# A four-layer graph network in fp32: layer 2's weight product by a seven-product scheme over two graphs, softmax weights turned in place, and smaller buffers

## The chip, the cores and the metric

The kernel runs on one core of one Trainium2 chip. The time is that of one execution on the device, in microseconds (us). The kernel before ran three times: median 2760.49 us, from 2757.43 to 2760.59. Engines are named as the profile names them: PE (matrix engine, with PEld for its weight loads), DVE (vector), ACT (scalar), POOL (GpSimd), SP (the queue that issues most DMAs). All data are fp32.

## The reference

There are 128 graphs of 128 nodes with 512 channels, one 128 x 128 weighted adjacency `adj`, and four layers. Each layer adds its result to its input and then normalises the row (`ln`: mean 0, variance 1, over the 512 channels).

```python
# x: (128 graphs, 128 nodes, 512 channels); adj: (128, 128)
# layer 0: A = adj @ x; the whole of it reduces to relu(max over channels of A + b) per node
x = ln(x + relu(max(adj @ x, axis=-1) + b)[..., None])
# layer 1: graph attention
h = x @ W; s1 = h @ a1; s2 = h @ a2
att = softmax(leaky_relu(s1[:, None] + s2[None, :]) * adj)
x = ln(x + elu(att @ h + beta * h))
# layer 2: graph convolution
y = adj @ x
x = ln(x + y @ weight + bias)
# layer 3: attention with 8 heads of 64, masked where adj == 0
q, k, v = x @ Wq + bq, x @ Wk + bk, x @ Wv + bv
x = ln(x + concat_heads(softmax(q @ k.T / 8 + mask) @ v))
```

## The kernel before

**Order of the work.** The kernel is written out as one instruction stream by a planner in Python (`Plan`, L23 to L133). Each stage of the work is a generator that announces what it will use: `dve(us)`, `act(us)`, `pool(us)`, `sp(us, landing)`, a buffer tag, or a mark of another stage. The planner keeps a clock for PE and one for each other engine with the costs that the code gives, and at each moment picks the PE stage with the smallest due place whose marks and buffers are there (L97 to L133). So each engine has one fixed order, and at run time every engine takes its instructions strictly in that order, waiting on semaphores. A stage's due place is `(graph + turns) * 7 + position in the row` (L955 to L960): in one round each graph-stage is done once, for graphs that lie up to some 15 apart.

**PE stages of one graph.** `l0` (L399) is adj x input, one product of 512 columns. `zT` (L503) is four products of 128 columns, `z` (L517 in `product`, called from `l1_out`) four of 512 columns accumulated in one PSUM bank, with the layer-1 weight as the moving operand and the turned data as the stationary one. `yT` (L560) and `y` (L517 again, called from `l2_out`) are the same pair for layer 2: `yT` holds (adj x2) turned, and `y` multiplies it by `w2_sb`. `xT`, or a turn by DMA and DVE, makes layer 3's input stationary.

**q, k, v by seven products.** For layer 3 the weight products of four graphs at a time (a group, GB = 4) are already made from seven products of half-size blocks (`seven`, L682 to L757; the tables `SEVEN` and `WAITS` at L668). The 512 x 512 weight is cut into four blocks, and so are the 512 nodes' data; sums and differences of blocks are made once for the weights (`weight_sums`, L327) and per group for the data (`token_sums`, L590, on POOL). A step is four matmuls of 256 columns. Steps 0, 2, 4, 5 accumulate in one bank (`chain`), step 1 in `first`, steps 3 and 6 in `pair`; between the steps ACT or DVE copy partial sums out, so that step 2 waits for the copy of step 0, step 4 for that of step 2, step 5 for that of step 4, and step 6 for a finished block.

**After `y`.** DVE adds `ps_y` and `x2b` (L605), where POOL has made `x2b = x2 + bias` before (L546). `layernorm` (L351 to L365) is bn_stats and bn_aggr on DVE (L354, L356), three small POOL instructions (L359, L361, L363) and one ACT pass (L365).

**Turns.** `turn` (L367 to L388) transposes a tile without PE: SP writes it to HBM, reads it back with rows regrouped, and DVE transposes 32 x 32 blocks (L386). The destination there is addressed with neighbouring elements four apart, which is 16 bytes. Layer 1's attention (n = 1), layer 3's input (n = 4), the softmax weights `pr` (n = 8, into a tile `turn8` and from there to `pT`) and the head outputs `oT` (n = 4) go this way.

**Softmax and `av`.** `l3_scores` (L794) makes 8 score products, DVE adds the mask (L816) and takes the maximum (L822), ACT makes 8 exponentials (L826); after the turn, `l3_avT` makes 16 half-height products (L880) whose moving operand is `pT[:, e * 4 + f, :]`, 128 elements side by side, and ACT copies them to `oT` (L892).

**PSUM.** Six banks (`mm`) serve all stages but the scores, which have two banks of their own as one tile.

Of the kernel before, what the change touches and what calls it, by code (L numbers as in the profile page):

```python
# [14 lines left out]
P = 128  # L15
# [121 lines left out]
def kernel(  # L137
# [30 lines left out]
        "x0": 2, "x1": 4, "x2": 2, "x2b": 2, "x3": 2, "x3r": 1, "xp": 4, "junk": 1,  # L168
        "s2_bc": 2, "s2_row": 2, "e": 2, "pe": 2, "att": 1, "attT": 2, "zT": 1, "yT": 1, "elu_r": 1,
        "xTh": 3, "T": 1, "st": 4, "qTh": 3, "kTh": 3, "pr": 1, "pT": 2, "oT": 1,  # L170
        "turn1": 2, "turn4": 2, "turn8": 1,
    }
    ps_bufs = {"mm": 6, "sc": 1}
    hbm_bufs = {"s2_hbm": 3, "turn_hbm1": 3, "turn_hbm4": 3, "turn_hbm8": 3, "x3_hbm": 16}
    NV = 2
# [96 lines left out]
    for i in range(NV):  # L272
        t = const.tile([P, GB, H, HD + 1], F32, tag=f"va{i}", name=f"va{i}")
        nc.vector.memset(t, 1.0)
        va_bufs.append(t)
# [13 lines left out]
    def w1_a():  # L289

        yield sp(0.0, 6.5)
        for i in (1, 0):
            junk = yield from get("junk", [P, C], f"wa_junk{i}")
            dg = yield from get("oT", [P, NCC, P], f"wa_diag{i}")
            yield dve(3.9)
            cols = small.tile([P, NCC], F32, tag="cols", name=f"wa_cols{i}")
            for c in range(NCC):
                nc.vector.scalar_tensor_tensor(
                    junk, w1_sb[:, c, :], 1.0, a_bc[i], ALU.mult, ALU.mult, accum_out=cols[:, c : c + 1]
                )  # L300
            nc.vector.tensor_tensor(
                dg,
                ident.unsqueeze(1).to_broadcast([P, NCC, P]),
                cols.unsqueeze(2).to_broadcast([P, NCC, P]),
                ALU.mult,
            )
            plan.give("junk")
            plan.give("xp")
            yield "mm"
            ps = ps_tile("mm", f"ps_wa{i}")  # L310
            yield ("PE", 1.0, 0.0)
            nc.tensor.matmul(ps, ones, dg.rearrange("p c n -> p (c n)"), start=True, stop=True)
            plan.give("oT")
            yield dve(0.7)
            nc.vector.tensor_copy(wa_bc[i], ps)
            plan.give("mm")
            plan.mark(("wa", i))
        yield dve(0.5)
        nc.vector.tensor_scalar(bq_s, bq_col, QS, None, ALU.mult)
        nc.vector.tensor_scalar(beta_id, ident, beta_col, None, ALU.mult)  # L320
        plan.mark("beta_id")
# [5 lines left out]
    def weight_sums(n, w):  # L327

        t = const.tile([P, 3, 2, HALF], F32, tag=f"sums_{n}", name=f"sums_{n}")
        a11, a12, a21, a22 = (w[:, 2 * c : 2 * c + 2, r * HALF : (r + 1) * HALF] for r in range(2) for c in range(2))  # L330
        sums[n] = (a11, a12, a21, a22, t[:, 0], t[:, 1], t[:, 2])
        yield sp(0.0, {"q": 44.0, "k": 52.0, "v": 60.0}[n])
        if n == "q":
            for c in range(NCC):
                yield act(0.6)
                nc.scalar.mul(w[:, c, :], w[:, c, :], QS)
        for dst, x_, y_, op in (
            (t[:, 0], a21, a22, ALU.add),
            (t[:, 1], t[:, 0], a11, ALU.subtract),
            (a21, a11, a21, ALU.subtract),  # L340
            (t[:, 2], a12, t[:, 1], ALU.subtract),
        ):
            yield pool(1.3)
            nc.gpsimd.tensor_tensor(dst, x_, y_, op)
            yield sp(0.0, 0.7)
        plan.mark(("sums", n))
# [20 lines left out]
    def turn(src, tag, place, n, name, kept="turn_hbm{}"):  # L367

        kept = kept.format(n)
        d = yield from get_hbm(kept, [NQ, P, n * Q], f"turn_hbm_{name}")
        yield sp(0.35, {1: 4.0, 4: 5.5, 8: 5.5}[n])
        nc.sync.dma_start(out=d.rearrange("b p x -> p b x"), in_=src.rearrange("p b n r -> p b (n r)"))
        plan.give(tag)
        t = yield from get(f"turn{n}", [P, NQ, n, Q], f"turn_{name}")
        yield sp(0.35, {1: 4.0, 4: 4.0, 8: 5.0}[n])
        nc.sync.dma_start(
            out=t.rearrange("p a n r -> p (a n r)"), in_=d.rearrange("b (c a) x -> (b c) (a x)", a=NQ)  # L380
        )
        if kept.startswith("turn"):
            plan.give(kept)
        dst = yield from place()
        yield dve({1: 0.3, 4: 0.7, 8: 1.25}[n])
        nc.vector.transpose(dst.rearrange("p n (c a) -> p a n c", a=NQ), t)  # L386
        plan.give(f"turn{n}")
        return d  # L388
# [5 lines left out]
    def l0(b):  # L394
# [11 lines left out]
        xp = yield from get("xp", [P, C], f"xp0_{b}")  # L406
        yield act(0.72)
        nc.scalar.activation(xp, xin_b, AF.Identity, bias=rl)
        plan.give("x0")
        if b + sb_bufs["x0"] < B:  # L410
            plan.at(plan.end, load_x(b + sb_bufs["x0"]))
        yield from layernorm(xp, x1, f"0_{b}")
        plan.give("xp")
        s["x1"] = x1
        cols = []
        for i in (1, 0):
            yield ("mark", ("wa", i))
            junk = yield from get("junk", [P, C], f"junk{i}_{b}")
# [3 lines left out]
                junk, x1, 1.0, wa_bc[i], ALU.mult, ALU.mult, accum_out=col  # L422
            )
            plan.give("junk")
# [95 lines left out]
    def l1_out(b):  # L520
# [23 lines left out]
        xb = yield from get("x2b", [P, C], f"x2b_{b}")  # L544
        yield pool(1.28)
        nc.gpsimd.tensor_tensor(xb, x2, bias2_bc, ALU.add)  # L546
        s["x2b"] = xb
        done_x2(b)

    def done_x2(b):  # L550
        st[b]["x2_uses"] = st[b].get("x2_uses", 0) + 1
        if st[b]["x2_uses"] == 2:
            plan.give("x2")

    def l2_yT(b):
        s = st[b]
        x2 = s.pop("x2")
# [5 lines left out]
        done_x2(b)  # L563
        yT = yield from get("yT", [P, C], f"yT_{b}")
        yield act(0.6)
        nc.scalar.copy(yT, ps)
        plan.give("mm")
        s["yT"] = yT
        plan.mark(("yT", b))

    xTh, xsum, heads = {}, {}, {}
    uses = {}
# [22 lines left out]
    def l2_out(b):  # L595
        s = st[b]
        yT = s.pop("yT")
        ps = product(f"y_{b}", lambda c: yT[:, c * P : (c + 1) * P], lambda c: w2_sb[:, c, :])
        plan.give("yT")
        if b == B - 1:  # L600
            plan.give("w")
            plan.give("w")
        xp = yield from get("xp", [P, C], f"xp2_{b}")
        yield dve(0.7)
        nc.vector.tensor_tensor(xp, ps, s.pop("x2b"), ALU.add)  # L605
        plan.give("mm")
        plan.give("x2b")
        x3 = yield from get("x3", [P, C], f"x3_{b}")
        early = b < EARLY
        x3_v = x3 if early else x3.rearrange("p (b n c) -> p b n c", b=NQ, c=Q)  # L610
        yield from layernorm(by_block(b, xp), x3_v, f"2_{b}")
        plan.give("xp")
        g, j = divmod(b, GB)
        half = j // 2
        if j % 2 == 0:
            xTh[g, half] = yield from get("xTh", [P, NCC, 2, P], f"xTh_{g}_{half}")
        if j == 0:
            plan.at(plan.end, token_sums(g))
        if early:
# [8 lines left out]
        place = lambda: made(xTh[g, half][:, :, j % 2, :])  # L628
        s["x3_hbm"] = yield from turn(x3_v, "x3", place, NCC, f"x3_{b}", "x3_hbm")
        plan.mark(("xT", b))  # L630

    def done_x3(b):
        st[b]["x3_uses"] += 1
        if st[b]["x3_uses"] == 2:
            plan.give("x3")
# [18 lines left out]
    def l3_xT(b):  # L654
# [6 lines left out]
        done_x3(b)  # L661
        yield act(0.6)
# [3 lines left out]


    SEVEN = ((0, 0), (1, 1), (5, 5), (2, 3), (4, 4), (6, 2), (3, 6))  # L668
    WAITS = (None, None, 1, 2, 0, None, 3)

    def seven(n):
        bias = {"q": bq_s, "k": bk_col}.get(n)

        def step(t):
# [3 lines left out]
            bank = ("chain", "first", "chain", "pair", "chain", "chain", "pair")[i]  # L678
# [19 lines left out]
            def out(r, c):  # L698

                if n == "v":  # L700
                    return va_bufs[g % NV][:, 2 * c : 2 * c + 2, 4 * r : 4 * r + 4, 0:HD]
# [30 lines left out]
            def half_tile(c):  # L732
                if n != "v":
# [43 lines left out]
    def seven_bufs(n):  # L777
        return lambda t: {"mm": 1 if t % 7 in (0, 1, 3) else 0, **({"va": 1} if n == "v" and t % 7 == 0 else {})}

    def seven_place(n):  # L780
        def at(t):
            g, i = divmod(t, 7)
            order = 14 + i if n == "v" else 2 * i + (n == "k")
            return (GB * g + 7.5 + order * GB / 21) * R
# [3 lines left out]
    def l3_scores(b):  # L788
# [53 lines left out]
        def place():  # L842
            s["pT"] = yield from get("pT", [P, H, P], f"pT_{b}")
            return s["pT"]

        yield from turn(pr_q, "pr", place, H, f"pr_{b}")
        plan.mark(("pT", b))

    def l3_pT(i):
# [11 lines left out]
        s["pT"] = sb_tile("pT", [P, H, P], f"pT_{b}")  # L861
# [10 lines left out]
    def l3_avT(b):  # L872
# [3 lines left out]
        va = va_bufs[b // GB % NV][:, b % GB]  # L876
        ps = ps_tile("mm", f"ps_av_{b}")
        for f in range(NCC):
            for e in range(2):
# [3 lines left out]
                    pT[:, e * 4 + f, :],  # L883
# [3 lines left out]
        if b % GB == GB - 1:  # L887
# [3 lines left out]
        yield act(0.62)  # L891
        nc.scalar.copy(oT.rearrange("p b n c -> p n b c"), ps.rearrange("p (n b c) -> p n b c", n=NCC, b=NQ))  # L892
# [23 lines left out]
    def l3_av(i):  # L916
# [4 lines left out]
        va = va_bufs[b // GB % NV][:, b % GB]  # L921
# [9 lines left out]
        else:  # L931
            if b % GB == GB - 1:
# [23 lines left out]
    turns = {"av": 14.5, "sc": 11.5, "yT": 3, "y": 3, "l0": 0, "zT": 2, "z": 2}  # L956
# [8 lines left out]
    def av_waits(b):  # L965
# [11 lines left out]
        "y": (place("y"), 3.45, lambda b: [("yT", b)], need("mm"), l2_out),  # L977
# [16 lines left out]
    total.update(s2=EARLY, attT=EARLY, xT=EARLY, pT=LATE, avT=B - LATE, av=2 * LATE, **{n: 7 * (B // GB) for n in "qkv"})  # L994
# [4 lines left out]
    for n, w in (("q", wq_sb), ("k", wk_sb), ("v", wv_sb)):  # L999
# [33 lines left out]
```

## Time and profile before

| | |
|---|---|
| median of 3 runs | 2760.49 us |
| the profiled execution: its time, its span | 2759.28 us, 2757.5 us |
| PE busy | 2707.9 us |
| DVE busy | 2248.3 us |
| ACT busy | 1578.1 us |
| POOL busy | 1391.1 us |
| DMA moved | 392.26 MB, mean 142 GB/s |
| `y` products (L517, 1024 records) | 466.7 us |
| q, k, v steps (L690): one group of 256 records, as `ps_q_first` | 60.5 us |

A record is one pass of a matmul: an fp32 matmul leaves two. A line of the profile names the source line, the engine, the operation, destination<-sources, the shapes, the number of records, and then the total busy time, the mean of one in ns, and the idle time of the engine just before. The ends of PE records are modelled and overlap the start of the next, so for PE the distance from start to start is the better duration. In the timeline, the columns are start, duration, engine, line.

### The profile page before, as it was taken

The numbers are of one execution on the slowest core, as the hardware profiler recorded it, in microseconds if no ns is written. First come the engines' busy times: TensorE is split into PE (matmuls) and PEld (weight loads), VectorE is DVE, ScalarE is ACT, GpSimd is POOL, SyncE is SP. The second block draws the span as 40 slices with busy tenths as digits, with TensorE's granted clock in tenths as the row PEclk, the third lists the DMA queues.
The fourth block names the chain that finished last, engine by engine and source line by source line (L and its number), as shares of the span: only waits on it lengthen the run. The fifth ranks groups of instructions, "written<-read, shape, count | busy, mean of one in ns | idle before, by whom it ended". The sixth has DMA issues, their size and how long they took to land.

```text
span 2757.5 us, 43085 instructions
## 1 busy us (share of the span) xinstructions
PE 2707.9 (98%) x13905; PEld 1936.6 (70%) x13905; DVE 2248.3 (82%) x4288; ACT 1578.1 (57%) x4189; POOL 1391.1 (50%) x2192
## 2 busy tenths in 40 slices
PE   6999999999999999999999999999999999999997
PEld 3677767777777777777777777777777777777776
DVE  7668888888888888888888888888888888888866
ACT  3445655655556555556555656555565655555555
POOL 3535445555455555455554555554545544555545
PEclk8999999999999999999999999999999999999998
DMA  3224444544544454445445444445545544454443
GB/s 124 60 72 149 149 144 147 152 150 142 150 146 141 158 147 145 155 142 153 149 138 159 147 148 147 148 147 152 152 137 153 153 142 148 146 156 145 141 148 111
DMA packets 459794, 392.26 MB, mean 142 GB/s; under 512 B 88752, under 2 KB 376624, under 8 KB 459568
## 3 DMA queue, kind: packets, MB, share of 16 engines
q1 hardware_dynamic: 456464, 383.74, 45.6%
q10 hardware_dynamic: 2976, 5.77, 0.6%
q8 instruction: 109, 1.79, 0.3%
q14 instruction: 117, 0.96, 0.1%
q0 software_dynamic: 128, 0.01, 0.0%
HBM read 218.17 MB, written 171.24 MB: 141 GB/s over the span
## 4 chain that ended last, share of the span: by engine, by line
PE 95%; DVE 2%; POOL 1%; DMA 1%; issue 0%; ACT 0%; SPq 0%; POOLq 0%; DVEq 0%
PE ps_y L517 16%; PE ps_z L517 16%; PE ps_v_chain L690 8%; PE ps_k_chain L690 8%; PE ps_q_chain L690 8%; PE ps_sc L794 5%; PE ps_yT L560 5%; PE ps_av L880 4%; PE ps_zT L503 4%; PE ps_q_pair L690 4%; PE ps_v_pair L690 4%; PE psA L399 4%; PE ps_k_pair L690 4%; PE ps_q_first L690 2%; PE ps_v_first L690 2%; PE ps_k_first L690 2%
## 5 line engine op out<-in xcount | busy, mean ns | idle before, releaser
L365 ACT ACTIVATE x<-xp,nmr,rstd 128x512 f32<-128x512 f32 x384 | 311.4, 811 | 348.8 <-POOL nmr L363 347.7
L359 POOL TENSOR_SCALAR ve<-mv 128x1 f32<-128x1 f32 x512 | 124.3, 243 | 732.7 <-DVE mv L356 487.3
L517 PE MATMUL ps_y<-w_sb,yT 128*128 128x512 f32 x1024 | 466.7, 598 | 0.0
L517 PE MATMUL ps_z<-w_sb,zT 128*128 128x512 f32 x1024 | 462.4, 594 | 3.8 <-DVE xp L605 2.6
L826 ACT ACTIVATE pr<-pr,nm 128x128 f32<-128x128 f32 x992 | 384.2, 391 | 120.3 <-DVE nm L822 117.3
L354 DVE BATCH_NORM_STATS2 stats<-xp 128x6 f32<-128x512 f32 x512 | 347.1, 678 | 49.4 <-POOL xp L906 22.2
L517 PEld LDWEIGHTS ps_z<-w_sb,zT 128*128 128x128 f32 x1024 | 194.4, 191 | 211.1 <-issue 202.1
L517 PEld LDWEIGHTS ps_y<-w_sb,yT 128*128 128x128 f32 x1024 | 188.4, 190 | 195.7 <-issue 191.0
L361 POOL TENSOR_TENSOR rstd<-ve,nhalf 128x1 f32<-128x1 f32 x512 | 296.1, 578 | 42.7
L648 POOL TENSOR_TENSOR x3r<-x3r,bv_bc 128x512 f32<-128x512 f32 x128 | 179.1, 1400 | 245.3 <-DMA x3r<-turn_hbm_x 235.2
L386 DVE STREAM_TRANSPOSE pT<-turn_pr 128x1024 f32<-128x1024 f32 x122 | 250.7, 2055 | 0.0
L421 DVE SCALAR_TENSOR_TENSOR junk<-x,wa_bc 128x512 f32<-128x512 f32 x256 | 228.4, 892 | 13.8 <-ACT x L365 12.6
L905 POOL TENSOR_TENSOR xp<-xp,rd 128x512 f32<-128x512 f32 x122 | 127.3, 1043 | 149.0 <-DVE xp L386 93.5
L534 DVE SCALAR_TENSOR_TENSOR xp<-ps_z,x 128x512 f32<-128x512 f32 x128 | 88.4, 691 | 123.0 <-ACT elu_r L530 120.8
L826 ACT ACTIVATION_READ_ACCUMULATOR pr<-pr,nm 128x1 f32 x976 | 184.3, 189 | 0.0
L546 POOL TENSOR_TENSOR x2b<-x,bias_bc 128x512 f32<-128x512 f32 x128 | 164.2, 1283 | 37.4 <-ACT x L365 37.1
L906 POOL TENSOR_TENSOR xp<-xp,x3r 128x512 f32<-128x512 f32 x122 | 169.7, 1391 | 9.6
L816 DVE TENSOR_TENSOR pr<-ps_sc,mask 128x1024 f32<-128x1024 f32 x124 | 151.0, 1218 | 23.7 <-PE ps_sc L794 22.8
L363 POOL TENSOR_SCALAR nmr<-mv,rstd 128x1 f32<-128x1 f32 x512 | 139.6, 273 | 53.0
L530 ACT ACTIVATE elu_r<-ps_z 128x512 f32<-128x512 f32 x128 | 75.3, 589 | 154.7 <-PE ps_z L517 154.5
L794 PEld LDWEIGHTS ps_sc<-kTh,qTh 64*128 64x128 f32 x2048 | 124.2, 187 | 49.2 <-issue 42.6
L503 PEld LDWEIGHTS ps_zT<-attT,x 128*128 128x128 f32 x1024 | 130.6, 193 | 29.7 <-issue 26.6
(148 smaller groups left out, 5816.9 us busy)
## 6 DMA issues: line engine op xcount, KB each, us to landing
turn_hbm_pr<-pr SPq DMA_DIRECT2D x122, 512.0 KB
turn_pr<-turn_hbm_pr SPq DMA_DIRECT2D x122, 512.0 KB
x<-in_x_dram SPq DMA_DIRECT2D x128, 256.0 KB
out_dram<-xp SPq DMA_DIRECT2D x128, 256.0 KB
turn_hbm_x<-x SPq DMA_DIRECT2D x124, 256.0 KB
turn_x<-turn_hbm_x SPq DMA_DIRECT2D x124, 256.0 KB
x3r<-turn_hbm_x SPq DMA_DIRECT2D x124, 256.0 KB
turn_hbm_o<-oT SPq DMA_DIRECT2D x122, 256.0 KB
```

The source lines that it names most:

```text
L354: nc.vector.bn_stats(stats, src)
L361: nc.gpsimd.tensor_tensor(rstd, ve, nhalf, ALU.pow)
L365: nc.scalar.activation(dst, src, AF.Identity, bias=nmr, scale=rstd)
L386: nc.vector.transpose(dst.rearrange("p n (c a) -> p a n c", a=NQ), t)
L421: nc.vector.scalar_tensor_tensor(junk, x1, 1.0, wa_bc[i], ALU.mult, ALU.mult, accum_out=col)
L503: nc.tensor.matmul(ps[:, c * P : (c + 1) * P], s["x1"][:, c * P : (c + 1) * P], attT, start=True, stop=True)
L517: nc.tensor.matmul(ps, lhsT(c), rhs(c), start=(c == 0), stop=(c == NCC - 1))
L648: nc.gpsimd.tensor_tensor(s["x3r"], s["x3r"], by_block(b, bv_bc), ALU.add)
L690: nc.tensor.matmul(ps[:, m, :], lhsT, rhs, start=fresh and m + k == 0, stop=m + k == 2, skip_group_check=not fresh)
L794: nc.tensor.matmul(ps[:, h % 2, f, :], heads["q", g][j // 2][r : r + HD, f, j % 2 * P : (j % 2 + 1) * P], heads["k", g][j // 2][r : r + HD ...
L826: nc.scalar.activation(pr_h[:, i], pr_h[:, i], AF.Exp, bias=nm[:, i : i + 1], accum_out=None if late else den[:, i : i + 1])
L906: nc.gpsimd.tensor_tensor(by_block(b, xp), by_block(b, xp), s.pop("x3r"), ALU.add)
```

## The change

**Layer 2.** `l2_out` goes; `y` becomes `l2_seven`, run once for two graphs in seven steps of two matmuls each (256 columns), with the tables of q, k and v. `yT` holds both graphs of a pair. After the second `yT` copy, `y_sums` makes four differences of 128 x 256 on POOL. `add_bias2` adds the bias to `x2` itself on POOL, after `yT` has been read. Steps 0, 2 and 4 are copied out by ACT and get a half of `x2` added on POOL (`temp`); DVE adds the rest (`finish`, four half adds for each pair). A fourth set of weight sums is made at the start (`y`), and the weight block that the sums replace is overwritten in `w2_sb`.

**Turns.** For the softmax weights, DVE transposes the tile that was loaded in place, all of it side by side. The columns of `pT` then stand in four runs of 32 (`pT[:, :, e * 4 + f, :]`), and the ACT copy to `oT` puts them in order, with neighbours 16 bytes apart.

**Buffers.** `x0` is normalised in place and also takes the unused output of the two row sums of layer 1, so it is held until both are done; before, it was free after the first ACT pass. `x3` lives in an `xp` tile. `v`'s tiles hold two graphs each, three of them instead of two tiles of four. `turn8`, `x2b`, `x3` and `junk` go. q, k, v, the scores and `av` are due one round later.

```diff
-        "x0": 2, "x1": 4, "x2": 2, "x2b": 2, "x3": 2, "x3r": 1, "xp": 4, "junk": 1,
+        "x0": 2, "x1": 4, "x2": 4, "x3r": 1, "xp": 4,
...
-    NV = 2
+    NV = 3
...
-        yield sp(0.0, {"q": 44.0, "k": 52.0, "v": 60.0}[n])
+        yield sp(0.0, {"y": 30.0, "q": 44.0, "k": 52.0, "v": 84.0}[n])
...
-        t = yield from get(f"turn{n}", [P, NQ, n, Q], f"turn_{name}")
+        t = yield from get("pT" if place is None else f"turn{n}", [P, NQ, n, Q], f"turn_{name}")
...
+        if place is None:
+            yield dve(1.25)
+            nc.vector.transpose(t.rearrange("p a n c -> p (a n c)"), t.rearrange("p a n c -> p (a n c)"))
+            return t
...
-        xp = yield from get("xp", [P, C], f"xp0_{b}")
         yield act(0.72)
-        nc.scalar.activation(xp, xin_b, AF.Identity, bias=rl)
-        plan.give("x0")
...
+        nc.scalar.activation(xin_b, xin_b, AF.Identity, bias=rl)
+        yield from layernorm(xin_b, x1, f"0_{b}")
...
-                junk, x1, 1.0, wa_bc[i], ALU.mult, ALU.mult, accum_out=col
+                xin_b, x1, 1.0, wa_bc[i], ALU.mult, ALU.mult, accum_out=col
...
+            if i == 0:
+                plan.give("x0")
...
+    def add_bias2(b):
+
+        x2 = st[b]["x2"]
         yield pool(1.28)
-        nc.gpsimd.tensor_tensor(xb, x2, bias2_bc, ALU.add)
...
+        nc.gpsimd.tensor_tensor(x2, x2, bias2_bc, ALU.add)
+        plan.mark(("x2b", b))
...
+    def y_sums(p):
+
+        t = yield from get("Ty", [P, 3, 2, P], f"Ty_{p}")
+        d = ys[p]
+        b11, b21, b12, b22 = (d["yT"][:, j, 2 * k : 2 * k + 2] for j in range(2) for k in range(2))
+        d["blocks"] = (b11, b21, b22, b12, t[:, 0], t[:, 1], t[:, 2])
+        for i, dst, x_, y_ in ((0, t[:, 0], b12, b11), (1, t[:, 1], b22, t[:, 0]), (2, b12, b22, b12), (3, t[:, 2], b21, t[:, 1])):
+            yield pool(0.72)
+            nc.gpsimd.tensor_tensor(dst, x_, y_, ALU.subtract)
+            plan.mark(("Ty", p, i))
...
+    def l2_seven(t):
+
+        p, i = divmod(t, 7)
+        d = ys[p]
+        w_i, x_i = SEVEN[i]
+        bank = BANKS[i]
+        fresh = i in (0, 1, 3)
+        if fresh:
+            d[bank] = ps_tile("mm", f"ps_y_{p}_{bank}")[:, :HALF]
+        ps = d[bank]
...
+        for k in range(2):
+            nc.tensor.matmul(ps, x_k[:, k], sums["y"][w_i][:, k, :], start=fresh and k == 0, stop=k == 1, skip_group_check=not fresh)
...
+        def temp(j, r):
+            tmp = yield from get("sty", [P, HALF], f"sty_{p}_{i}")
+            yield act(0.36)
+            nc.scalar.copy(tmp, ps)
+            plan.mark(("y", p, i))
+            yield ("mark", ("x2b", 2 * p + j))
+            yield pool(0.72)
+            nc.gpsimd.tensor_tensor(tmp, tmp, half(j, r, "x2"), ALU.add)
...
+        def finish(j, r, key):
+            yield ("mark", ("y", p, key, "b"))
+            yield dve(0.45)
+            bank = d["first" if i == 1 else "pair"]
+            nc.vector.tensor_tensor(xp_half(j, r), as_xp(j, bank), as_xp(j, d.pop(("st", key))), ALU.add)
...
+        if i in (2, 4, 5):
+            keys.append(("y", p, {2: 0, 4: 2, 5: 4}[i]))
+        if i == 6:
+            keys.append(("y", p, "C", 1, 1))
...
-                    pT[:, e * 4 + f, :],
+                    pT[:, :, e * 4 + f, :],
...
-        yield act(0.62)
-        nc.scalar.copy(oT.rearrange("p b n c -> p n b c"), ps.rearrange("p (n b c) -> p n b c", n=NCC, b=NQ))
+        yield act(0.95)
+        nc.scalar.copy(oT.rearrange("p b n (l a) -> p n a b l", a=NQ), ps.rearrange("p (n a b l) -> p n a b l", n=NCC, a=NQ, b=NQ))
...
-    turns = {"av": 14.5, "sc": 11.5, "yT": 3, "y": 3, "l0": 0, "zT": 2, "z": 2}
+    turns = {"av": 15.5, "sc": 12.5, "yT": 3, "y": 3, "l0": 0, "zT": 2, "z": 2}
...
-        "y": (place("y"), 3.45, lambda b: [("yT", b)], need("mm"), l2_out),
+        "y": (
+            lambda t: place("y")(t // 7 * 2 + 1) + t % 7 * 0.3, 0.88, l2_waits,
+            lambda t: {"mm": 1 if t % 7 in (0, 1, 3) else 0}, l2_seven,
+        ),
```

## The prediction

> **What bounds the kernel now.** I read the page first, for busy shares and for the chain that ended last, then the stretches of the span, then PE's timeline in the steady middle.
>
> ```profile
> PE 2707.9 (98%) x13905; PEld 1936.6 (70%) x13905; DVE 2248.3 (82%) x4288; ACT 1578.1 (57%) x4189; POOL 1391.1 (50%) x2192
> ...
> PE 95%; DVE 2%; POOL 1%; DMA 1%; issue 0%; ACT 0%; SPq 0%; POOLq 0%; DVEq 0%
> ```
>
> PE is busy for all but 49.6 us of 2757.5, and 95% of the chain that ended last is PE. The stretches (length, then busy time and records of PE, PEld, DVE, ACT, POOL, then granted clock) say where the 49.6 us lie:
>
> ```profile
> 0.00:60.00 60.00, 35.40 (x92) 17.23 (x93) 41.86 (x111) 21.06 (x40) 17.47 (x34) 0.83 0.41 142
> 60.00:120.00 60.00, 54.30 (x217) 33.44 (x217) 41.09 (x92) 27.51 (x51) 42.31 (x59) 1.00 0.18 47
> 1200.00:1600.00 400.00, 400.00 (x2057) 286.22 (x2056) 339.50 (x636) 234.81 (x632) 200.19 (x320) 1.00 0.48 148
> 2680.00:2760.00 80.00, 60.93 (x446) 52.70 (x444) 50.69 (x83) 39.51 (x109) 44.57 (x58) 0.88 0.36 117
> ```
>
> Some 30 us are at the start, 19 at the end, nothing in between: in the middle PE does not wait, at full clock. So PE work that goes comes off the time one for one, and other engines' work is free until it makes PE wait. The timeline of PE gives prices from start to start:
>
> ```profile
> 1218.81 3.70 PE L517 MATMUL ps_y<-w_sb,yT 128*128 128x512 f32 x8
> 1222.34 1.05 PE L503 MATMUL ps_zT<-attT,x 128*128 128x128 f32 x8
> 1223.23 1.89 PE L690 MATMUL ps_q_pair<-T,wq_sb 128*128 128x256 f32 x8
> 1224.96 3.60 PE L517 MATMUL ps_z<-w_sb,zT 128*128 128x512 f32 x8
> 1228.39 1.89 PE L690 MATMUL ps_k_pair<-T,wk_sb 128*128 128x256 f32 x8
> 1230.12 1.89 PE L690 MATMUL ps_v_chain<-wv_sb,xTh 128*128 128x256 f32 x8
> ```
>
> Here `y` costs 3.53, `z` 3.43 and a step of four 256-column matmuls 1.73. Over 400 to 2600 us the mean of the whole `y` products in the timeline is 3.477, and of steps followed by a step 1.73, so half a step is 0.865. A wide matmul ahead of a 128-column one costs 0.09 more (a step before the scores 1.82, `l0` 0.95 against 0.86).
>
> **The change, part by part.**
>
> *The seven products.* Away go 128 x 3.477 = 445 us. In come 7 x 64 = 448 half steps, 448 x 0.865 = 387.5 us. The order of the changed program has 241 places where a wide product stands before a narrow one, against 208 before; 58 of the 208 were `y`'s and are already in the 3.477, so 241 - 150 = 91 are to be paid at 0.09, 8 us. Sum on PE: 387.5 + 8 - 445 = -49.5 us. All of this is on the path. Weight loads do not take over: the steps of q, k and v load one weight for each 256 columns too, 190 ns (PEld rows of L690) under passes of 0.216.
>
> *What feeds the new steps.* For each pair ACT makes three copies of 256 columns; 128 columns cost it 262 ns (L493), 512 cost 580 (L566), so about 0.37 each, 192 x 0.37 = 71 us. POOL makes four differences and three adds of 256 columns; 512 cost it 1.28 (L546) to 1.40 (L648), so about 0.7 each, 448 x 0.7 = 314 us, and POOL rises from 1391 to 1705 us, 63%. DVE makes four adds of 256 from PSUM; 512 cost 690 ns (L605), 256 cost 424 (L939), so 4 x 0.424 - 2 x 0.690 = +0.32 for each pair, +20 us. None of it is on the path while the steps find their data. Where PE could wait, by the changed order: from the second `yT` to step 2 lie 3.5 to 10.8 us of PE work, median 6.5, for an ACT copy of 0.58, two differences of 0.7 and the hand-overs, about 2.3; from step 4 to step 5 lie 1.73 in 53 pairs of 64 (0.87 in three), for one copy of 0.37; from step 4 to step 6 a median of 4.8, at least 1.9, for copy, POOL add and DVE add, about 1.8 together. Steps 4 and 5 of q stand 1.73 apart as well, with two ACT passes of 0.47 between, and PE does not wait. So bare durations fit; queues in front of ACT, POOL and DVE are what is left. I take 3 us of new waits, from 0 to 30 (0.5 for each pair).
>
> *POOL against DVE.* The timeline shows what more POOL work does to DVE:
>
> ```profile
> 1223.33 1.28 POOL L648 TENSOR_TENSOR x3r<-x3r,bv_bc 128x512 f32<-128x512 f32 x1 [3.42 <-DMA x3r<-turn_hbm_x]
> 1224.09 1.06 DVE L421 SCALAR_TENSOR_TENSOR junk<-x,wa_bc 128x512 f32<-128x512 f32 x1
> 1225.69 0.67 DVE L421 SCALAR_TENSOR_TENSOR junk<-x,wa_bc 128x512 f32<-128x512 f32 x1
> ```
>
> The same row sum takes 1.06 beside a POOL add and 0.67 without. About 800 DVE instructions read two SBUF tensors (L421, L536, L462, L463, L476); 314 us of 2710 are 12% of the time, and a hit waits half of 0.7, which is some 30 us in all. DVE with this and the +20: 2300 us, 85%. Free as long as DVE catches up.
>
> *The turn of the softmax weights in place.* The rows:
>
> ```profile
> L386 DVE STREAM_TRANSPOSE pT<-turn_pr 128x1024 f32<-128x1024 f32 x122 | 250.7, 2055 | 0.0
> L816 DVE TENSOR_TENSOR pr<-ps_sc,mask 128x1024 f32<-128x1024 f32 x124 | 151.0, 1218 | 23.7 <-PE ps_sc L794 22.8
> L438 DVE STREAM_TRANSPOSE s_row<-s 128x32 f32<-128x32 f32 x124 | 23.4, 189 | 0.0
> ```
>
> A turn of 1024 to places 16 bytes apart takes 2055 ns, 1.7 times an add of 1024. The Trainium skill (SBUF — State Buffer, section "Door 1: The DMA port swizzle") says that SBUF works in lines of 16 bytes, and that every access that crosses to a new line pays; by that the in-place turn, side by side, would come down to the 1.2 of the add: 122 x 0.85 = -104 us on DVE. Against it, the one turn that is side by side already, 32 wide, takes 189 ns, which lies on the straight line through the strided ones (373, 1116, 2055 for 128, 512, 1024): by that row the gain is nothing. I take the rule, since 32 elements are too few to tell a slope; DVE is then at 2200 us, 81%, and at 2300 without. The same rule speaks against the copy to `oT`, which now writes 16 bytes apart: at 580 ns now, it could double its slope of 0.83 ns an element, to 1.0 us; +0 to +52 us on ACT, which with the copies comes to 1650 to 1700, 61 to 63%. Neither end is on the path.
>
> *The new form of `pT` for PE.* The moving operand of `av` comes in four runs of 128 bytes. No matmul in the trace reads so. Nearest, the DVE add L816 writes runs of 32 elements at 1218 ns against 1191 for L822, and the ACT copy L892, in runs of 32 too, takes the 580 of L566: no price. Upper bound 25 ns on each of 1952 passes, a fifth of their distance, 49 us; below zero is excluded, as the same columns pass. I take 0.
>
> *Buffers, start and end.* The number of DMAs is the same, and a turn still takes 512 KB out and in. `x0` is held through the normalisation and two row sums, some 10 us in place of 3, with two tiles and a new graph each 21 us: free in the middle. At the start graphs 2 and 3 are loaded only after the row sums of 0 and 1, some 10 us later than now (psA of graph 2 at 17.5 us); PE idles there anyway until 45 us. Against that, the order brings 49 us of PE work before the first q step where it was 42. At the end the last scores stand closer together. I take 0 for both, and 10 us each way. PSUM gets tighter: the chain bank is held for some 20 us of each pair in place of one bank for 3.5, six in all; in the trace PE waits for a bank behind L605 for 2.6 us in total. This is in the 0 to 30.
>
> *Sum.* 2759.3 (profiled execution, 1.8 of it outside the span) - 49.5 + 3 = 2712.8; the median of the runs is 1.2 above the profiled one. Predicted: 2713.
>
> **The rivals.**
>
> *Feeders late, but not by much.* ACT, POOL and DVE stand behind one another between steps 4 and 6, and each has its own queue: eight exponentials hold ACT for 3.1 us. At 0.4 us for each pair, 64 x 0.4 = 26 us: 2736. For it: three engines in a row for a few us of cover. Against: q's steps have the same cover and no wait.
>
> *POOL blocks PE, slower.* POOL takes its instructions in order, and it now makes steps 2, 3, 4 and 6 possible. It stands waiting for `x3r` from DMA for 235.2 us in 77 waits, 3.1 each, up to 5.8; the differences of a pair may stand behind one, and then also behind adds of 1.4. Cover is 6.5 - 2.3 = 4.2 in the median and 1.2 at the least. It decides when PE loses more than 49.5 / 64 = 0.77 us for each pair; at 1.0 it is 2713 - 3 + 64 = 2774. Against: `token_sums` already feeds PE from POOL, with no wait in the middle of the span.
>
> *The gain is eaten, no change.* If the runs of `pT` cost the full 25 ns, 2713 + 49 = 2762, within the bound; or if half steps cost more than half of a step: 0.11 us more on 448 does the same. `l0`, one 512-column matmul in two passes, 0.86 for as many columns as a half step has, speaks against the second.
>
> **How the numbers follow.** PE stays the bound, 2713: 0.74, from 2698 (start and end both better, no waits) to 2727. Feeders late, 2736: 0.13. No change, 2762: 0.06. POOL blocks, 2774: 0.07. A measurement of this kernel can tell about 0.2%, 5.5 us, from no change. Faster: 0.74 + 0.13 = 0.87; same 0.06; slower 0.07. The range of 8 in 10 takes the first case and most of the second: 2698 to 2738.
>
> **What would show it.** PE busy near 2660 and the seven `y` groups summing to about 390 us; PE at full busy time in the middle stretches. In-place turns at 1.2 us, the `oT` copy up to 1.0. Idle time before `ps_y` matmuls released by ACT or DVE, or before any PE work by POOL, would show the feeders; `av` farther apart than 1.03 the runs of `pT`. The prediction is wrong if DVE goes beyond 90%, or if PE's idle time at the start grows well beyond 30 us.

## The result and the profile after

| | before | changed kernel |
|---|---|---|
| median | 2760.54 us (4 runs, 2757.43 to 2761.01) | 2714.4 us (4 runs, 2713.79 to 2714.82) |
| ratio | | 0.9835, 95% interval 0.9818 to 0.9852 |
| profiled execution: time, span | 2759.28, 2757.5 us | 2713.79, 2712.0 us |
| PE busy | 2707.9 us | 2653.9 us |
| span less PE busy | 49.6 us | 58.1 us |

The predicted 2713 is 1.4 us off. The span fell by 45.5 us: PE's busy time by 54.0, while its idle time grew by 8.5. The page of the changed kernel, busy shares and the chain that ended last:

```profile
PE 2653.9 (98%) x14673; PEld 2076.4 (77%) x14673; DVE 2234.2 (82%) x4417; ACT 1694.8 (62%) x4381; POOL 1710.9 (63%) x2644
...
PE 93%; DVE 2%; POOL 2%; issue 1%; ACT 0%; DMA 0%; SPq 0%; POOLq 0%; DVEq 0%; ACTq 0%
```

PE is still the bound. POOL has risen by 320 us and ACT by 117, while DVE, with the cheaper turn, but four half adds for each pair in place of two whole ones, has fallen by 14. The stretches of the changed kernel (columns as before the change) show where PE idles:

```profile
0.00:60.00 60.00, 32.58 (x102) 16.94 (x102) 43.08 (x113) 21.99 (x42) 25.38 (x40) 0.86 0.42 137
60.00:120.00 60.00, 49.52 (x212) 34.54 (x213) 41.24 (x94) 27.69 (x53) 51.02 (x71) 0.97 0.18 50
1200.00:1600.00 400.00, 400.00 (x2216) 314.26 (x2215) 340.66 (x671) 257.09 (x675) 259.26 (x404) 1.00 0.48 149
2640.00:2720.00 80.00, 54.03 (x418) 47.48 (x416) 46.77 (x81) 41.24 (x114) 42.46 (x57) 0.91 0.35 114
```

In the first 120 us PE idles for 27.4 + 10.5 = 37.9 us, where it was 24.6 + 5.7 = 30.3. That is 7.6 of the 8.5. The last stretch reaches 8 us beyond the end of the span, so 18.0 us of it are idle; before, the last 72 us had 16.6. The middle is full, and POOL there has gone from 200 to 259 of 400 us. In the middle (400 to 2600 us) these are all of PE's waits (total us, number, longest):

```profile
PE ps_y_chain L628 <- POOL Ty L584: 1.2, 2, 0.9
PE ps_yT L560 <- ACT x L365: 0.7, 1, 0.7
```

So the new steps find their data: three waits, 1.9 us in 2200. The rows behind the prediction's single prices (busy time, mean ns of one, idle before it), the last one from the kernel before:

```profile
L584 POOL TENSOR_TENSOR Ty<-yT,Ty 128x256 f32<-128x256 f32 x128 | 106.0, 828 | 1.5
L584 POOL TENSOR_TENSOR yT<-yT 128x256 f32<-128x256 f32 x64 | 51.5, 805 | 0.0
L584 POOL TENSOR_TENSOR Ty<-yT 128x256 f32<-128x256 f32 x64 | 49.4, 772 | 1.6 <-PE ps_y_pair L628 0.5 <-ACT yT L570 0.5
L657 POOL TENSOR_TENSOR sty<-sty,x 128x256 f32<-128x256 f32 x192 | 147.7, 769 | 222.4 <-ACT sty L653 203.6
L1003 ACT COPY oT<-ps_av 128x512 f32<-128x512 f32 x122 | 133.2, 1092 | 55.3 <-PE ps_av L991 53.2
L387 DVE STREAM_TRANSPOSE turn_pr<-turn_pr 128x1024 f32<-128x1024 f32 x122 | 150.7, 1235 | 13.1 <-DMA turn_pr<-turn_hbm_pr 12.9
...
L892 ACT COPY oT<-ps_av 128x512 f32<-128x512 f32 x122 | 70.8, 580 | 55.8 <-PE ps_av L880 52.7 <-issue 2.1 <-ACT w_sb L826 0.2
```

The in-place turn takes 1235 ns where the turn to places 16 bytes apart took 2055. The copy to `oT`, which now writes 16 bytes apart, takes 1092 ns where it took 580.

### The profile page after: what moved, and what is told of

The parts are those of the page before. It is cut to its first block, busy times and chain, and to the rows that moved or that the text cites. A ratio compares the mean times of both kernels' runs of the same rounds, so it can differ in the third digit from the quotient of the medians.

```text
span 2712.0 us, 45528 instructions
## 1 busy us (share of the span) xinstructions
PE 2653.9 (98%) x14673; PEld 2076.4 (77%) x14673; DVE 2234.2 (82%) x4417; ACT 1694.8 (62%) x4381; POOL 1710.9 (63%) x2644
## 4 chain that ended last, share of the span: by engine, by line
PE 93%; DVE 2%; POOL 2%; issue 1%; ACT 0%; DMA 0%; SPq 0%; POOLq 0%; DVEq 0%; ACTq 0%
PE ps_z L519 15%; PE ps_k_chain L803 8%; PE ps_q_chain L803 8%; PE ps_y_chain L628 8%; PE ps_v_chain L803 8%; PE ps_sc L909 5%; PE ps_zT L505 4%; PE ps_av L991 4%; PE ps_yT L560 4%; PE ps_k_pair L803 4%; PE ps_y_pair L628 4%; PE ps_v_pair L803 4%; PE ps_q_pair L803 4%; PE psA L404 4%; PE ps_v_first L803 2%; PE ps_q_first L803 2%
## 5 line engine op out<-in xcount | busy, mean ns | idle before, releaser
L941 ACT ACTIVATE pr<-pr,nm 128x128 f32<-128x128 f32 x992 | 386.2, 392 | 51.9 <-DVE nm L937 24.6
L354 DVE BATCH_NORM_STATS2 stats<-xp 128x6 f32<-128x512 f32 x384 | 258.3, 673 | 49.8 <-POOL xp L1017 41.2
L657 POOL TENSOR_TENSOR sty<-sty,x 128x256 f32<-128x256 f32 x192 | 147.7, 769 | 222.4 <-ACT sty L653 203.6
L755 POOL TENSOR_TENSOR x3r<-x3r,bv_bc 128x512 f32<-128x512 f32 x128 | 174.8, 1366 | 162.5 <-DMA x3r<-turn_hbm_x 154.9
L365 ACT ACTIVATE xp<-xp,nmr,rstd 128x512 f32<-128x512 f32 x256 | 206.5, 810 | 94.0 <-POOL nmr L363 82.4
L420 DVE SCALAR_TENSOR_TENSOR x<-x,wa_bc 128x512 f32<-128x512 f32 x256 | 223.9, 875 | 29.0 <-ACT x L365 25.8
L551 POOL TENSOR_TENSOR x<-x,bias_bc 128x512 f32<-128x512 f32 x128 | 165.3, 1291 | 89.9 <-PE ps_yT L560 64.6
L363 POOL TENSOR_SCALAR nmr<-mv,rstd 128x1 f32<-128x1 f32 x512 | 142.7, 279 | 53.0
L1003 ACT COPY oT<-ps_av 128x512 f32<-128x512 f32 x122 | 133.2, 1092 | 55.3 <-PE ps_av L991 53.2
L387 DVE STREAM_TRANSPOSE turn_pr<-turn_pr 128x1024 f32<-128x1024 f32 x122 | 150.7, 1235 | 13.1 <-DMA turn_pr<-turn_hbm_pr 12.9
L391 DVE STREAM_TRANSPOSE xTh<-turn_x 128x512 f32<-128x512 f32 x124 | 137.4, 1108 | 25.6 <-DMA turn_x<-turn_hbm_x 25.6
L560 PEld LDWEIGHTS ps_yT<-adjT,x 128*128 128x128 f32 x1024 | 130.3, 191 | 34.4 <-ACT x L365 17.9
L407 DVE TENSOR_REDUCE mx<-psA 128x1 f32<-128x512 f32 x128 | 87.8, 686 | 82.9 <-PE psA L404 82.7
```

The lines of the kernel that those rows point to most:

```text
L354: nc.vector.bn_stats(stats, src)
L365: nc.scalar.activation(dst, src, AF.Identity, bias=nmr, scale=rstd)
L420: nc.vector.scalar_tensor_tensor(xin_b, x1, 1.0, wa_bc[i], ALU.mult, ALU.mult, accum_out=col)
L551: nc.gpsimd.tensor_tensor(x2, x2, bias2_bc, ALU.add)
L560: nc.tensor.matmul(ps[:, c * P : (c + 1) * P], x2[:, c * P : (c + 1) * P], adjT, start=True, stop=True)
L755: nc.gpsimd.tensor_tensor(s["x3r"], s["x3r"], by_block(b, bv_bc), ALU.add)
```

## The experiments

All times are medians, and "the changed kernel" is 2714.4 us. Theory: PE is the bound, the time falls by the PE work that goes, and the other engines' work is free as long as PE finds its data. Rival: one of those engines, POOL or DVE, is so near its limit that its work reaches PE.

**What each half of the change is worth.** The first run keeps everything but the seven products: `y` is again one product for each graph.

```diff
-        "y": (
-            lambda t: place("y")(t // 7 * 2 + 1) + t % 7 * 0.3, 0.88, l2_waits,
...
+        "y": (place("y"), 3.45, lambda b: [("yT", b)], need("mm"), l2_out),
...
-    for n, w in (("y", w2_sb), ("q", wq_sb), ("k", wk_sb), ("v", wv_sb)):
+    for n, w in (("q", wq_sb), ("k", wk_sb), ("v", wv_sb)):
```

> The changed kernel with layer 2's weight product whole again, one graph at a time in four matmuls of 512 columns; the turn in place, the shared buffers and the later due places stay. Theory (all of the gain is PE passes that went): PE gets its 50 us back and the time is 2755 to 2765. Rival (a part of the gain is DVE's cheaper turn or the buffers): 2735 to 2750. If the longer idle time at the start came with the half steps and their POOL work, the time is near 2756, at the lower end; if with the buffers, near 2764.

Measured: 2761.0 us (13 runs), ratio to before 1.0007 (0.9999 to 1.0016). The seven products are worth 46.6 us, and the rest of the change together comes to nothing.

The second run puts the in-place turn alone into the kernel before.

```diff
-        t = yield from get(f"turn{n}", [P, NQ, n, Q], f"turn_{name}")
+        t = yield from get("pT" if place is None else f"turn{n}", [P, NQ, n, Q], f"turn_{name}")
...
+            nc.vector.transpose(t.rearrange("p a n c -> p (a n c)"), t.rearrange("p a n c -> p (a n c)"))
...
-                    pT[:, e * 4 + f, :],
+                    pT[:, :, e * 4 + f, :],
```

> The kernel before with one part of the change: the softmax weights are turned in place, av reads them in four runs of 32, and the oT copy writes 16 bytes apart. Theory (nothing of this is on the path): DVE busy falls by 100 us to about 2145, ACT rises by 60, and the time stays within 2756 to 2765. Rival (DVE at 82% costs PE time): 2740 or less. Rival (runs of 32 cost PE): 2770 or more, with av farther apart than 1.03.

Measured: 2752.0 us (9 runs), ratio 0.9974 (0.9965 to 0.9984). The time fell by 7 us, more than the forecast's nothing and less than a DVE on the path would give. These are the waits of the kernel before between 400 and 2600 us, and all of them are gone:

```profile
PE ps_z L517 <- DVE xp L605: 2.1, 4, 0.6
```

That is under a third of the 7 us. The planner, with its new costs, also puts PE's stages in another order in part, so turn and order are not separated here, and where the rest comes from stays open. The rest of the change (buffers, later places for layer 3) takes those 7 us back, since the first run stands 9 us above this one. Which part of it does was not tried.

**Where the 8 us at the start come from.** The forecast had named the held `x0` as the risk there. In the next run graphs 2 and 3 are loaded at once, into tiles that lie free.

```diff
-        x0[b] = yield from get("x0", [P, C], f"x0_{b}")
+        x0[b] = yield from get("x2" if b in (2, 3) else "x0", [P, C], f"x0_{b}")
...
-    for b in range(sb_bufs["x0"]):
+    for b in range(4):
```

> The changed kernel; graphs 2 and 3 of x are loaded at once, into tiles of x2 that stand empty at the start, so that they need not wait for the row sums of graphs 0 and 1. If the 8 us of PE idle time that were added in the first 120 us come from the held x0 tiles: 2705 to 2709, with PE idle near 30 us in the first 120. If they come from POOL, full from 53 to 93 us: 2712 to 2716.

Measured: 2716.9 us; PE idles for 38.0 us in the first 120. The held `x0` is not the cause.

The other suspect was the weight sums on POOL, so they were started earlier.

```diff
-        yield sp(0.0, {"y": 30.0, "q": 44.0, "k": 52.0, "v": 84.0}[n])
+        yield sp(0.0, {"y": 18.0, "q": 24.0, "k": 30.0, "v": 84.0}[n])
```

> The changed kernel; the weight sums of y, q and k are due at 18, 24 and 30 us instead of 30, 44 and 52, when POOL stands idle. If the added 8 us at the start come from POOL, which is full from 53 to 93 us: 2704 to 2709, with less PE idle time between 60 and 90 us than the 10.5 of the changed kernel. If they come from the held x0 tiles: 2712 to 2716.

Measured: 2718.5 us; PE idles for 38.3 us in the first 120, less from 60 on and more before. The sums only change place in a queue that is full. So the work itself had to leave that stretch: graphs 0 to 3 take the whole `y` product, the seven steps begin with the third pair, and `y`'s weight sums wait for the whole products.

```diff
+        "yw": (place("y"), 3.45, lambda b: [("yT", b)], need("mm"), l2_out),
...
-            lambda t: place("y")(t // 7 * 2 + 1) + t % 7 * 0.3, 0.88, l2_waits,
+            lambda t: place("y")(t // 7 * 2 + 1 + EARLY) + t % 7 * 0.3, 0.88, l2_waits,
```

> The changed kernel, but graphs 0 to 3 take the whole y product as before, and the seven steps begin with the third pair; y's weight sums are made only after the whole products. Theory (the first pairs of seven steps, with their weight sums and differences on a POOL that is busy without a gap from 53 to 93 us, delay the first q step from 79.5 to 97.8 us and cost the 7.8 us that PE loses at the start): the loss in the first 120 us falls from 49.7 back to about 42 us, the first q step comes near 80 us, PE gets 4 x 3.477 - 14 x 0.867 = +1.8 us more work, so 2714.4 - 7.8 + 1.8 = about 2708. Rival (the loss is that of the held x0 and the later graphs, or of POOL's other work there, and not of the seven steps): 2714 to 2718, the first q step stays past 90 us.

Measured: 2708.45 us (2706.65 to 2710.51), ratio to before 0.9814 (0.9801 to 0.9827), as expected, and faster than both kernels, than the changed one by 6 us (their runs do not overlap). Its stretches at the start:

```profile
0.00:60.00 60.00, 33.79 (x99) 17.39 (x100) 41.27 (x110) 20.32 (x38) 17.29 (x35) 0.86 0.40 132
60.00:120.00 60.00, 54.76 (x226) 35.17 (x225) 44.89 (x102) 30.84 (x59) 49.59 (x64) 1.00 0.21 55
```

PE idles for 26.2 + 5.2 = 31.4 us, 6.5 less than in the changed kernel, and POOL has 8 us less to do in the first 60. The first step of q starts at 77.4 us; it was 97.8 in the changed kernel and 79.5 before. So the first pairs of the seven products are what costs most of the 8 us. PE's waits of the first 120 us say through what: those of the `y` products themselves fall from 2.9 to 0.9 us, and those of `yT` for the normalised `x2` (L365) from 6.6 to 3.0. In the changed kernel POOL, from 53 to 93 us, stands idle only once, for 0.5 us. That its full queue carries the loss is argued and not shown, for here too it has hardly a pause between 54 and 80 us. `y`'s weight sums, 5.5 us of POOL, move too, from 37 to 44 us in the changed kernel to 86 to 96 us here. They were not tested alone, but in the changed kernel they lie ahead of the full stretch.

**How near DVE is.** In the next run DVE turns the first 320 columns of the softmax tile twice more, which gives the same tile. It stands, roughly, for the change without the cheaper turn.

```diff
             nc.vector.transpose(t.rearrange("p a n c -> p (a n c)"), t.rearrange("p a n c -> p (a n c)"))
+            h = t.rearrange("p a n c -> p (a n c)")[:, 0:320]
+            nc.vector.transpose(h, h)
+            nc.vector.transpose(h, h)
```

> The changed kernel, where DVE turns the first 320 columns of the softmax weights' tile twice more in place (which gives the same tile again): about 2 x 0.42 us for each graph, 122 x 0.84 = +103 us on DVE, with one input and no second tensor read, so each turn costs DVE the 2.07 us that it cost before the change. It stands for the change without the cheaper turn. Theory A (DVE's load reaches PE in proportion, as the heavier pass showed with 46 us for 170 us): 2714.4 + 103 x 46/170 = about 2742. Theory B (only what exceeds some 90% of the middle stretches counts, or the price of the heavier pass was its two-tensor read beside POOL): 2716 to 2725. The forecast's own step had put it at nothing: 2714.

Measured: 2733.9 us (2732.99 to 2739.06), 19.5 us above the changed kernel. The forecast's step ("neither end is on the path") falls. One extra turn took 511 ns where 420 were expected, so DVE's busy time is up by 117 us, and not by the 100 that the in-place turn had saved. Two heavier doses: 512 columns twice more, and a pass over the whole tile that reads two tensors.

```diff
+            h = t.rearrange("p a n c -> p (a n c)")[:, 0:512]
+            nc.vector.transpose(h, h)
+            nc.vector.transpose(h, h)
```

> As the last, but 512 columns twice more: about 2 x 0.65 us for each graph, +159 us on DVE, nearly the load of the heavier pass, but with one input. If the price of the heavier pass was DVE's load and queue: 2750 to 2758. If it was the read of two tensors, which holds POOL up (x3r adds 1607 ns against 1424): 2720 to 2735.

```diff
+            nc.vector.tensor_tensor(t, t, t, ALU.max)
```

> The changed kernel, with one more DVE pass of 128 x 1024 (a maximum of the tile with itself, which changes nothing) behind each in-place turn: DVE gets 122 x 1.2 = about 150 us more, 2234 to about 2385 us (88%), which is more than the 104 us that the contiguous turn saved. Theory (DVE is off the path and the cheaper turn by itself is worth nothing): 2714 to 2717. Rival (the turn alone on the kernel before gave 7.4 us because DVE's load does reach PE through the adds behind z and y): 2720 to 2728, with PE waits behind DVE adds in the middle of the span.

| DVE work added, by the trace | time | over the changed kernel | us for each us |
|---|---|---|---|
| 117 us (turn's cost back) | 2733.9 us | 19.5 us | 0.17 |
| 161 us (one input) | 2745.4 us | 31.0 us | 0.19 |
| 178 us (two inputs) | 2760.1 us | 45.7 us | 0.26 |

The smallest dose brings DVE to 86% of the span (89% between 400 and 2600 us), and each us of it costs 0.17 us already; where below that the price begins was not measured. With the heaviest one all that the change gains is gone. Two rows of that run, from its page, tell why it is dearer than its load:

```profile
L756 POOL TENSOR_TENSOR x3r<-x3r,bv_bc 128x512 f32<-128x512 f32 x128 | 205.6, 1607 | 182.2 <-DMA x3r<-turn_hbm_x 173.4
...
L658 POOL TENSOR_TENSOR sty<-sty,x 128x256 f32<-128x256 f32 x192 | 160.6, 836 | 185.5 <-ACT sty L654 177.1
```

POOL's own adds have grown (1607 against 1366 ns, 836 against 769) and its busy time by 58 us, although it does nothing more. With one input POOL's busy time stayed at 1706 us. The three largest of PE's waits in the middle (400 to 2600 us), with two inputs and then with one (161 us):

```profile
PE ps_yT L561 <- ACT x L365: 12.0, 13, 1.9
PE ps_y_chain L629 <- POOL Ty L585: 7.5, 13, 1.3
PE ps_y_pair L629 <- POOL yT L585: 3.1, 5, 1.2
```

```profile
PE ps_y_pair L631 <- DVE xp L668: 8.2, 13, 1.0
PE ps_yT L563 <- ACT x L365: 5.7, 11, 0.8
PE ps_v_pair L806 <- DVE va L841: 1.9, 2, 1.7
```

With two inputs PE waits mostly for POOL's differences and for the normalisation, and for DVE by name only 3.7 us in six waits: DVE's delay comes to it through the others. With one input it waits first of all for DVE's own adds of the seven steps (L668), and for the differences only 1.4 us. All three doses stand at one place, behind the turn; another place was not tried, but no wait of `av` for the turned tile stands among PE's waits there.

**How near POOL is.** Behind the bias add, POOL takes the bias off `x2` and adds it again; the values stay the same. Half of the columns first, then all, once and twice:

```diff
         nc.gpsimd.tensor_tensor(x2, x2, bias2_bc, ALU.add)
+        nc.gpsimd.tensor_tensor(x2[:, 0:HALF], x2[:, 0:HALF], bias2_bc[:, 0:HALF], ALU.subtract)
+        nc.gpsimd.tensor_tensor(x2[:, 0:HALF], x2[:, 0:HALF], bias2_bc[:, 0:HALF], ALU.add)
```

> The changed kernel, with two more POOL passes of 128 x 256 for each graph behind the bias add (the bias is taken off and added again in half of the columns): half the load of the run with two passes of 512, which cost 289 us; POOL gets about 128 x 1.5 = +190 us. If the price is proportional: 2714 + 289 x 190/333 = about 2880. If there is a threshold that the pair's 4 us of cover sets: 2730 to 2800.

```diff
         nc.gpsimd.tensor_tensor(x2, x2, bias2_bc, ALU.add)
+        for _ in range(1):
+            nc.gpsimd.tensor_tensor(x2, x2, bias2_bc, ALU.subtract)
+            nc.gpsimd.tensor_tensor(x2, x2, bias2_bc, ALU.add)
```

> The changed kernel, with two more POOL passes of 128 x 512 for each graph (the bias is taken off and added once more), POOL from 1711 to about 2040 us (75%). Theory (POOL has slack enough to feed the seven steps): 2714 to 2725, the loss at the start somewhat larger, the middle nearly without waits. Rival (POOL blocks PE, the mechanism of the forecast's slower case, is near): 2740 or more, with PE waits behind POOL in the middle.

The next is the same with `range(2)`.

> The changed kernel, with four more POOL passes of 128 x 512 for each graph, POOL to about 2370 us (87%). Theory: here the slack is gone, POOL's waits for DMA (about 3 us each) leave no room, and PE waits behind POOL in the middle: 2740 to 2800. If POOL could be filled without a price as long as its own sum stays under PE's: 2714 to 2730.

And the load of one full pair of passes in another place, where no step of layer 2 needs the result:

```diff
         nc.gpsimd.tensor_tensor(by_block(b, xp), by_block(b, xp), s.pop("x3r"), ALU.add)
+        nc.gpsimd.tensor_tensor(xp, xp, bias2_bc, ALU.subtract)
+        nc.gpsimd.tensor_tensor(xp, xp, bias2_bc, ALU.add)
```

> The changed kernel, with two more POOL passes of 128 x 512 for each graph in another place: behind layer 3's residual add, ahead of the last normalisation (the bias of layer 2 is taken off and added again, which leaves the values). The load is that of the run that took 3003 us, but nothing in layer 2 waits for these instructions by data; they only stand in POOL's queue. If the place set the price (bias adds right ahead of a pair's differences): 2720 to 2780. If POOL's queue as a whole has no room: 2900 or more.

| POOL work added, by the trace | POOL's share | time | over the changed kernel | us for each us |
|---|---|---|---|---|
| 198 us, half the columns | 67% | 2832.6 us | 118 us | 0.60 |
| 312 us, late in layer 3 | 69% | 2919.8 us | 205 us | 0.66 |
| 333 us, at the bias add | 68% | 3003.0 us | 289 us | 0.87 |
| 648 us, at the bias add | 68% | 3453.1 us | 739 us | 1.14 |

Every expectation that left POOL room is missed by far. POOL is at its limit with two thirds of its time busy: more work makes the span longer, and the share stays at 67 to 69%. The late place costs 205 us too, so most of it is the queue as a whole and not what stands ahead of a pair's differences. Not all of the price is waiting: PE's granted clock, 0.994 in the changed kernel, is 0.991, 0.981, 0.971 and 0.919 in the four rows, and PE is busy for 2688, 2717, 2754 and 2896 us with the work that took it 2654. So the rising price of the last rows is partly a PE that runs slower.

PE's waits with the smallest dose (400 to 2600 us), and one of them followed through the timelines of PE, ACT and POOL:

```profile
PE ps_z L519 <- ACT zT L511: 36.3, 39, 1.9
PE ps_y_chain L630 <- POOL Ty L586: 29.4, 31, 2.2
```

```profile
1243.42 3.70 PE L519 MATMUL ps_z<-w_sb,zT 128*128 128x512 f32 x8 [1.85 <-ACT zT L511]
```

```profile
1242.08 0.81 ACT L365 ACTIVATE xp<-xp,nmr,rstd 128x512 f32<-128x512 f32 x1 [2.17 <-POOL nmr L363]
1242.80 0.56 ACT L511 COPY zT<-ps_zT 128x512 f32<-128x512 f32 x1
```

```profile
1237.27 1.37 POOL L551 TENSOR_TENSOR x<-x,bias_bc 128x512 f32<-128x512 f32 x1
1238.71 0.73 POOL L552 TENSOR_TENSOR x<-x,bias_bc 128x256 f32<-128x256 f32 x1
1239.53 1.05 POOL L553 TENSOR_TENSOR x<-x,bias_bc 128x256 f32<-128x256 f32 x1
1240.67 0.22 POOL L359 TENSOR_SCALAR ve<-mv 128x1 f32<-128x1 f32 x1
1240.97 0.71 POOL L361 TENSOR_TENSOR rstd<-ve,nhalf 128x1 f32<-128x1 f32 x1
1241.79 0.26 POOL L363 TENSOR_SCALAR nmr<-mv,rstd 128x1 f32<-128x1 f32 x1
```

Read from below: POOL spends 3.2 us on the three bias passes and then 1.2 on the normalisation's small instructions. ACT stands idle for 2.17 us at the pass that needs them. The copy of `zT` stands behind that pass in ACT's queue, though the `zT` product began at 1238.68 and takes 1.0. PE waits 1.85 us for the copy. No instruction in this chain belongs to the seven products, and none but the bias passes is new. It is the rule and not one case: of the 39 waits for `zT` in that stretch, 38 lead back through ACT's queue to a pass of L365 that waited for POOL (L363).

## Why the prediction was right, and where it was not

**PE's sum: right.** Forecast -49.5 us; PE's busy time fell by 54.0. Over 400 to 2600 us a half step takes 0.867 us from start to start (0.865 in the sum), so 448 of them are 388 us. The 8 us for places where a wide product stands before a 128-column one were too general. The changed kernel's timeline has `l0` ahead of the scores, and ahead of a `zT`:

```profile
1164.89 1.02 PE L404 MATMUL psA<-x,adjT 128*128 128x512 f32 x2
1165.85 1.16 PE L909 MATMUL ps_sc<-kTh,qTh 64*128 64x128 f32 x16
...
1210.00 1.02 PE L404 MATMUL psA<-x,adjT 128*128 128x512 f32 x2
1210.86 1.05 PE L505 MATMUL ps_zT<-attT,x 128*128 128x128 f32 x8
```

Before the scores it takes 0.96 from start to start, before `zT` 0.86, which is its price without the extra. Between 120 and 2640 us all 92 wide products ahead of the scores pay the 0.09, and only 8 of the 128 ahead of a `zT` or `yT`. What PE does beside `y` did grow, though: summed from start to start, `zT` by 7.5 us and `l0` by 3.3, while `yT` fell by 5.6, which is 5 us for the new order in place of 8.

**New waits, 3 us: right in the middle.** Three waits, 1.9 us, are what the trace shows there.

**Start and end, taken 0, from -10 to 10: the mis-sized term.** The start cost 7.6 us of idle PE. It lay within the bound but had the wrong cause beside it: early loads did not help (2716.9), and taking the first two pairs out did (2708.45). The sum came out within 1.4 us because PE's busy time fell 4.5 us more than forecast and its idle time grew 5.5 us more: two errors that nearly cancel, which is luck. (The "19 at the end" before were 16.6 us, since that stretch reached beyond the span's end; the forecast did not use it.)

**POOL's feeding, 314 us: 13% too low.** The three rows of L584 and the row of L657 sum to 355 us. The median add is 728 ns, near the 0.7 taken, but the mean is 769 and the differences have 772 to 828. The forecast charged what POOL and DVE do to each other to DVE alone. Its total for POOL, 1705 us, came near the measured 1711 because POOL's other rows fell by 35 us, which it had not foreseen.

**POOL against DVE, 30 us on DVE: less than half of what came.** Four small instructions of layer 1 took 351, 361, 350 and 386 ns before and take 475, 506, 485 and 508; over 124 to 128 graphs that alone is 67 us. One of them before and after, and one case of it beside POOL:

```profile
L476 DVE SCALAR_TENSOR_TENSOR att<-pe,rd,beta_id 128x128 f32<-128x128 f32 x128 | 49.4, 386 | 5.4 <-DVE rd L475 0.2
L478 DVE SCALAR_TENSOR_TENSOR att<-pe,rd,beta_id 128x128 f32<-128x128 f32 x128 | 65.0, 508 | 5.1 <-DVE rd L477 0.4
```

```profile
1238.20 1.16 DVE L478 SCALAR_TENSOR_TENSOR att<-pe,rd,beta_id 128x128 f32<-128x128 f32 x1
```

```profile
1237.72 1.49 POOL L755 TENSOR_TENSOR x3r<-x3r,bv_bc 128x512 f32<-128x512 f32 x1 [3.06 <-DMA x3r<-turn_hbm_x]
```

POOL's add ends at 1239.21 and this one 0.15 us later. It takes 1.16 us; the same instruction takes 0.35 at 1275.15, with no such add beside it. Over the whole trace, 174 of these four instructions' 512 records overlap a wide POOL pass, and take 0.87 us in the mean; the others take 0.30. In the kernel before, 55 of 512 overlapped one.

**The turn: its duration right, its worth wrong.** The rule of the Trainium skill (SBUF — State Buffer, section "Door 1: The DMA port swizzle"), chosen over the row of the 32-wide turn, gave 1.2 us and -104 us on DVE; measured are 1235 ns and -100. By the same rule `oT` was to reach 1.0 us; it takes 1.09. The sizes fit the rule, but no run here tries the spacing alone (the turn is now in place as well). That this is worth nothing on the path is the step that failed. "Free as long as DVE catches up" supposes a threshold, set at 90%. The runs show a price below it: putting 117 us back on DVE, which brings it from 82% to 86% of the span, takes 19.5 of the 46 us. For the 100 us of the turn itself that is some 17 us (an estimate at the same rate). In the kernel before, the same turn gave 7. So the forecast's equality of PE work removed and time gained would not have held without the turn.

**The new form of `pT`: right.** From the start of an `av` to what follows it are 1.024 us, as before. That is eight products with two records each (not the sixteen products of the text on the kernel before), so records stand 0.064 us apart. The upper bound of 25 ns on each was two fifths of that, not a fifth.

**The rivals.** "POOL blocks PE" did not come, but its price lay no more than 198 us of POOL work away. Its mechanism is what the loaded runs show, with one difference: it acts through the normalisation and ACT's queue (`zT` behind L365) as much as through the pair's differences. 198 us more, which is 3.1 for each pair, cost 1.85 for each pair; that would have made the change slower than the kernel before. Where between 0 and 198 us the price begins was not measured. The argument for room, POOL at 63% and no waits, was true of the changed kernel and said nothing of its reserve.

## What to carry to other kernels

Price work that leaves the bounding engine one for one, but ask of each engine that feeds it what one more us costs, and measure that with a dose that changes no result: POOL, which feeds three engines in a fixed order and waits in between, stood at 63% here and got no higher than 69%, whatever was added. Look for a saving on such a feeder before adding to it: the cheaper turn, worth 7 us alone, was worth some 17 beside the seven products. Where a pipeline fills, leave out the scheme that needs the full feeder: whole products for the first four graphs gave the fastest kernel of the study, 2708.45 us.

## What was not expected of the hardware

- A DVE pass with two tensors from SBUF slows POOL as POOL slows DVE: with 122 such passes added, POOL's busy time grew by 58 us for the same instructions. Turns with one input, 161 us of work on DVE, left it at 1706 us.
- Writing 16 bytes apart was dear on two engines: DVE's turn of 1024 elements 2055 against 1235 ns, ACT's copy of 512 elements 1092 against 580.
- A turn of 320 columns side by side takes 511 ns and one of 1024 takes 1235, 1.03 ns for each further element.
